# One ring of three PSUM slots, and one carry addition for two scans, in a selective-scan layer

## The chip, the core and the metric

The kernel runs on one core of one Trainium2 chip. A core has five engines with a queue of instructions each: PE (TensorE, matrix products, which writes to PSUM only), DVE (VectorE), ACT (ScalarE), POOL (GpSimd) and SP (SyncE, which here issues DMAs). Each engine works through its queue in order, and engines wait for each other by semaphores: an instruction may raise a count when it ends, and another may wait until the count has reached a value. The metric is the device time of one execution in microseconds (us).

The kernel is written in a language that records instructions and works out the semaphores itself, from which tiles an instruction reads and writes. Tiles come from pools: a pool with three buffers hands out three memory areas in turn, and a new tile waits until the last user of its area is done. Where the program asks for a manual schedule, the order on the engines named is the order of the code; elsewhere a scheduler orders them.

## What is computed

Four layers run one after the other on x (4 images of 64 x 64 pixels, 128 channels). The change is in layer 0, a state-space layer. Its heart is a scan over the 4096 pixels of an image, in four directions (rows, columns, and both backwards), for 256 inner channels with 16 states each:

```python
def step(h, inp):
    u_i, d_i, b_i, c_i = inp
    dA = jnp.exp(d_i[..., None] * A)
    h = h * dA + (d_i * u_i)[..., None] * b_i[:, None, :]
    y = jnp.einsum('gdn,gn->gd', h, c_i)
    return (h, y)
...
xs = jnp.stack([x_flat, x_t, jnp.flip(x_flat, 1), jnp.flip(x_t, 1)], axis=1)
...
ys = _selective_scan(xs, dts4, A, Bp4, Cp4, D_param, b_dt)
```

So h is multiplied by a decay dA and gets a product of the input (d times u) and b added; y sums h times c over the states. Ahead of it stand a group norm, a projection and a 3 x 3 convolution, behind it a layer norm, a gate and a projection.

## The kernel before

**Chunks and halves.** Layer 0 takes an image as 64 chunks of 64 steps, for two halves of the channels (128 each): 4 images x 2 halves x 64 chunks = 512 rounds of one loop (`for I in range(N)`). In a round c is the chunk's number, h the half. All four directions of a chunk are worked in the same round: j = 0, 1 (forwards, backwards) and kp = 0, 1 (rows, columns).

**One round** has two pairs, kp = 0 and kp = 1. For each:

- `products(q, kp)` (line 655) takes two PSUM tiles from the pool `db`, of 16 x 64 float32 a partition each (two PSUM banks), one for each j, and fills them with the products of `du` (d times u) and the diagonal tiles `dg` (b). These are 16 small matmuls on PE, which the trace shows as 32 records (two each): half 0 has four for j = 0 and then four for j = 1, then comes a drain of PE, then half 1 with four for j = 0 and four for j = 1. The tile of j = 0 is complete at the 12th matmul, that of j = 1 at the 16th.
- `scan(I, q, kp, bs, st, old, new)` (line 678), on DVE: for each j it adds the carry `old` (the last state of the chunk before, times the first decay) to the first of the 64 columns of the PSUM tile (line 684, 128 x 16 elements; not where c is 0), and runs the scan of 1024 elements (line 687) from the PSUM tile and the decays dA into `st` (tile `big` in SBUF). Then POOL makes the carry for the next round (line 694, `cy`) and multiplies both scans' states by c (line 702).

The pool `db` has three buffers (line 175), so the two tiles of the next pair get the third buffer and the one that the first scan of the present pair reads.

**Around it.** `inputs` (line 644) computes `du` on DVE for the next round. `total` (line 722) sums the states over n on PE, for the round two before; ACT copies the sums out (line 736). `diagonal` (line 636) and `decay` (line 591) make dg and dA on ACT. `beside` runs the other stages for the neighbouring images (`back`, `front`, `middle`, and `also` for layer 1's spectra), a step at a time, between the pairs; these use one PSUM tile of their own (`bg`).

**Order.** In the loop PE, ACT and DVE are under a manual schedule: PE has products (kp = 0), half of `total`, a step of `beside`, products (kp = 1), a step of `beside`, the other half of `total`; DVE has the scans (kp = 0), du, and what the step of `beside` has for it, the scans (kp = 1), and again a step. POOL and SP are ordered by the scheduler.

**Ahead of the loop** `front` and `middle` of image 0 run by themselves, ordered by the scheduler, and take their PSUM tiles one bank at a time from the same pool `db` (`turn_bank`, line 754).

Of the kernel before, what the change touches and what calls it, by code (L numbers as in the profile page):

```python
# [9 lines left out]
ALU = mybir.AluOpType  # L10
AX = mybir.AxisListType
PSUM = bass.MemoryType.PSUM
DRAM = bass.MemoryType.DRAM

P = 128
# [5 lines left out]
BLK = 512  # L21
# [6 lines left out]
TC = 64  # L28
NCHUNK = S // TC
NH0 = NST // 2  # L30
# [29 lines left out]
def tl(pool, shape, tag, dtype=F32, bufs=None):  # L60
    return pool.tile(shape, dtype, name=tag, tag=tag, bufs=bufs)
# [99 lines left out]
def layer0(cm, x, W, x1, also, kept):  # L161


    tc, nc = cm.tc, cm.nc
    wl = kept.enter_context(tc.tile_pool(name="l0k", bufs=1))
    dr = kept.enter_context(tc.tile_pool(name="l0dram", bufs=2, space=DRAM))
    with ExitStack() as ctx:
# [4 lines left out]
        t4 = ctx.enter_context(tc.tile_pool(name="l0t4", bufs=4))  # L172
        yb = ctx.enter_context(tc.tile_pool(name="l0y", bufs=2))
        p2 = ctx.enter_context(tc.tile_pool(name="l0p2", bufs=2))
        db = ctx.enter_context(tc.tile_pool(name="l0db", bufs=3, space=PSUM))
        pp = ctx.enter_context(tc.tile_pool(name="l0pp", bufs=1, space=PSUM))

        w_in = tl(wp, [P, 4 * P], "w_in")
# [58 lines left out]
        for i in range(2):  # L237
            t = tl(wp, [P, QC, 2, NH0, TC], f"dA{i}")
# [12 lines left out]
        for i in range(2):  # L251
            t = tl(wp, [P, 8, PADW], f"padded{i}")
            nc.vector.memset(t, 0.0)
            padded.append(t)
        for h in range(2):
            frame = xc_d[4 * h : 4 * h + 4].rearrange("g p s -> (g p) s")
            line = padded[h].rearrange("p r w -> p (r w)")
            nc.sync.dma_start(frame[:, 0:PADW], line[:, 0:PADW])
            nc.sync.dma_start(frame[:, (PADW - 1) * PADW :], line[:, 0 : PADW + 2])
        dg_d = tl(dr, [NCHUNK, P, NST * QR], "dg_d", bufs=1)  # L260

        img = {}
# [289 lines left out]
        def place(I):  # L552
            u, c = divmod(I, NCHUNK)
            return divmod(u, 2) + (c,)
# [100 lines left out]
            )  # L655

        def products(q, kp):
            bs = [tl(db, [P, 2 * NH0, TC], "db") for _ in range(2)]
            mm = None
            for half in range(2):  # L660
                if half:
                    nc.tensor.drain()
                for i in range(8):
                    j, r, p = i // 4, i // 2 % 2, i % 2
                    g = r ^ half
                    rows = slice((2 * j + r) * QR, (2 * j + r + 1) * QR)
                    t0 = (r ^ j) * QR
                    nc.tensor.matmul(  # L668
                        bs[j][
                            p * TC : (p + 1) * TC, g * NH0 : (g + 1) * NH0, t0 : t0 + QR  # L670
                        ],
                        lhsT=q["du"][rows, kp, g * TC : (g + 1) * TC],
                        rhs=q["dg"][rows, p * NH0 : (p + 1) * NH0, :],
                        start=True, stop=True,
                    )
            return bs

        def scan(I, q, kp, bs, st, old, new):
            c = q["c"]
            us = slice(2 * kp, 2 * kp + 2)  # L680
            for j in range(2):
                u = 2 * kp + j
                if c:
                    nc.vector.tensor_tensor(  # L684
                        bs[j][:, :, 0], bs[j][:, :, 0], old[:, u, :], ALU.add
                    )
                nc.vector.tensor_tensor_scan(  # L687
                    st[:, u].rearrange("p n t -> p (n t)"),
                    q["w"]["dA"][:, c % QC].rearrange("p g n t -> p (g n t)"),
                    bs[j].rearrange("p n t -> p (n t)"),  # L690
                    0.0, ALU.mult, ALU.add,
                )
            if c + 1 < NCHUNK:
                nc.gpsimd.tensor_tensor(  # L694
                    new[:, us, :], st[:, us, :, TC - 1],
                    quads[(I + 1) // QC]["a0"][:, (c + 1) % QC]
                    .rearrange("p g n -> p (g n)").unsqueeze(1)
                    .to_broadcast([P, 2, 2 * NH0]),
                    ALU.mult,
                )  # L700
            sv = st[:, us].rearrange("p j (g n) t -> p (j g) (n t)", g=2)
            nc.gpsimd.tensor_tensor(  # L702
                sv, sv,
                q["ct"].rearrange("p n t -> p (n t)").unsqueeze(1)
                .to_broadcast([P, 4, NH0 * TC]),
                ALU.mult,
            )

        def total(I, part):
# [36 lines left out]
            if c % (NCHUNK // 2) == NCHUNK // 2 - 1:  # L746
                for r in range(2):
# [3 lines left out]
                        ys[2].rearrange("p r w -> p (r w)")[:, rows], accum_op=ALU.add,  # L751
                    )

        def turn_bank():
            return tl(db, [P, BLK], "db")

        def own_bank():
            return tl(pp, [P, BLK], "bg")
# [5 lines left out]
        for _ in run(front(0, turn_bank), middle(0, turn_bank, t4, "t4k", 2)):  # L764
            pass
# [21 lines left out]
        with tc.manual_schedule(engines=engines):  # L787
            for I in range(N):
                b, h, c = place(I)
# [26 lines left out]
                if I + 1 < N:  # L816
                    nxt = start(I + 1)
                    diagonal(nxt)
                bs = products(now, 0)
                scan(I, now, 0, bs, st, carry, new)  # L820
                if nxt:
                    inputs(nxt)
# [5 lines left out]
                if w:  # L828
                    if c % QC == 1:
                        begun(w)  # L830
                    if c % QC == 2:
                        first(w)
                    decay(w, c % QC)
                bs = products(now, 1)
                scan(I, now, 1, bs, st, carry, new)
                if beside:
                    next(beside, None)
# [1432 lines left out]
def hybrid_kernel(tc, I, cst, out):  # L2270
    def part(prefix):
        return {k[len(prefix) :]: v for k, v in I.items() if k.startswith(prefix)}

    nc = tc.nc
    x = I["x"].rearrange("b r w c -> b (r w) c")
    out = out.rearrange("b r w c -> b (r w) c")
    with ExitStack() as ctx:
        cm = Common(ctx, tc, cst)
        dram = ctx.enter_context(tc.tile_pool(name="x1", bufs=1, space=DRAM))
        x1 = tl(dram, [B, S, D], "x1")  # L2280
        sp_d = tl(dram, [P, NT // UT, 5, UT, C], "sp_d")

        def also(*a):
            return spectra(cm, part("L1_conv_"), cst, sp_d, *a)

        xa = tl(dram, [B, S, D], "xa")
        xh_d = tl(dram, [B, S, D], "xh_d")
        lg_d = tl(dram, [P, 2, S], "lg_d")
        with ExitStack() as kept:
            last = layer0(cm, x, part("L0_conv_"), x1, also, kept)  # L2290
            recurrence_and_attention(
                cm, x1, part("L1_conv_"), part("L2_attn_"), part("L2_ffn_"), sp_d, xa, xh_d,
                lg_d, last,
            )
        x2 = tl(dram, [B, S, D], "x2")
        experts(cm, part("L2_ffn_"), xa, xh_d, lg_d, x2)
        layer3(cm, part("L3_attn_"), part("L3_ffn_"), cst, x2, out)
# [59 lines left out]
```

## Time and profile before

| What | us |
|---|---|
| Median of 3 runs | 10801.76 (10794.61 to 10804.73) |
| The profiled execution's own time | 10775.49 |
| Its span, first instruction to last | 10773.7 |
| DVE busy in the span | 7683.5 |
| PE busy in the span | 8887.1 |
| POOL busy in the span | 5462.3 |
| Scans (line 687), first to last start | 342.3 to about 6173 |

A trace's row names a line, an engine, an operation, the tile written and the tiles read, the shape and a count; behind it stand busy time and mean duration, or, in a timeline, start and duration in us. In square brackets, or behind the second bar, stands the idle time of the engine just before, with what ended it. Matmul records overlap in PE's pipeline, so their durations don't add up; what counts is when the first starts and when the engine behind it starts.

### The profile page before, as it was taken

To read this page: it belongs to the slowest core of one execution; us is meant where nothing else is said; L and a number is where in the kernel's file an instruction comes from. 1 tells how busy PE (TensorE), PEld (TensorE's weight loads), DVE (VectorE), ACT (ScalarE), POOL (GpSimd) and SP (SyncE) were. 2 spreads that over 40 slices of the span, in tenths; PEclk is the share of its full clock that TensorE was granted. 3 is DMA by queue.
4 is the path that set the end of the run, shared out by engine and by line. 5 is a ranking of instruction groups with operands and counts; after the bars stand their busy time and mean duration, and the time that the engine had idled before them with its cause. 6 is when DMAs were issued, how large, how long until landed. Compare 5 with 4: busy or idle time off the path is not lost. (4 is left out here: it accounts for less than half of the span.)

```text
span 10773.7 us, 190011 instructions
## 1 busy us (share of the span) xinstructions
PE 8887.1 (82%) x72040; PEld 4203.6 (39%) x72040; DVE 7683.5 (71%) x10667; ACT 5321.0 (49%) x13151; POOL 5462.3 (51%) x2661
## 2 busy tenths in 40 slices
PE   6678998779887788887788746999999956988886
PEld 2233443334333333333333323444444434544442
DVE  1699999999889999999999975636361132455546
ACT  5557554556444564445532124767676613433321
POOL 0579999889888888888999920000000000000000
PEclk7789998889888898888889868999999976687766
DMA  5434554335443344543333231111100083112101
GB/s 151 104 95 129 145 140 111 105 110 152 132 121 108 109 125 136 136 117 104 100 94 92 74 113 39 36 35 40 30 27 16 16 226 72 29 35 59 39 20 47
DMA packets 1155618, 960.91 MB, mean 89 GB/s; under 512 B 191940, under 2 KB 905384, under 8 KB 1148312
## 3 DMA queue, kind: packets, MB, share of 16 engines
q1 hardware_dynamic: 1140888, 898.41, 29.0%
q0 software_dynamic: 13824, 50.34, 2.6%
q8 instruction: 579, 9.49, 0.4%
q14 instruction: 327, 2.68, 0.1%
HBM read 616.68 MB, written 331.61 MB: 88 GB/s over the span
## 5 line engine op out<-in xcount | busy, mean ns | idle before, releaser
L687 DVE TENSOR_TENSOR_SCAN big<-dA,db 128x1024 f32<-128x1024 f32 x2048 | 4680.1, 2286 | 82.9 <-PE db L668 4.7
L702 POOL TENSOR_TENSOR big<-big,ct 128x2048 f32<-128x2048 f32 x1024 | 4653.7, 4545 | 78.8 <-POOL cy L694 0.4
L668 PE MATMUL db<-dg,du 32*64 32x256 f32 x32768 | 1914.5, 423 | 770.0 <-DVE db L684 625.4
L722 PE MATMUL yp<-big,both 128*64 128x256 f32 x16384 | 2368.4, 438 | 59.6 <-ACT yc L736 49.6
L722 PEld LDWEIGHTS yp<-big,both 128*64 128x64 f32 x16384 | 1250.5, 155 | 1158.8 <-issue 762.6
L668 PEld LDWEIGHTS db<-dg,du 32*64 32x64 f32 x32768 | 657.1, 136 | 2001.7 <-issue 1912.8
L736 ACT COPY yr<-yp 128x64 f32<-128x64 f32 x1024 | 224.6, 220 | 1538.0 <-PE yp L722 1537.6
L1480 PE MATMUL av<-e,x 128*128 128x512 f32 x2048 | 974.0, 592 | 4.6 <-ACT e L1475 4.6
L1431 PE MATMUL qk<-a,xT 128*128 128x512 f32 x2048 | 966.6, 594 | 8.7 <-ACT e L1435 7.9
L1435 ACT ACTIVATE e<-qk,nk 128x512 f32<-128x512 f32 x1024 | 694.0, 686 | 537.4 <-PE qk L1431 535.5
L591 ACT ACTIVATE dA<-dp,A 128x252 f32<-128x252 f32 x2048 | 869.6, 504 | 93.9 <-issue 48.7
L636 ACT ACTIVATE dg<-mask,BT 128x32 f32<-128x32 f32 x4096 | 902.2, 328 | 5.2 <-PE db L668 5.2
L1010 POOL TENSOR_TENSOR g_rs<-g_rs,qrow 128x4 f32<-128x4 f32 x32 | 41.2, 1286 | 1499.9 <-DVE g_rs L1009 1499.9
L694 POOL TENSOR_TENSOR cy<-big,a 128x32 f32<-128x32 f32 x1008 | 348.0, 345 | 467.3 <-DVE big L687 393.6
L1431 PEld LDWEIGHTS qk<-a,xT 128*128 128x128 f32 x2048 | 378.0, 190 | 462.4 <-issue 358.0
L1480 PEld LDWEIGHTS av<-e,x 128*128 128x128 f32 x2048 | 381.6, 190 | 434.8 <-issue 394.6
L1475 ACT ACTIVATE e<-e 128x1024 f32<-128x1024 f32 x510 | 539.4, 1058 | 15.4
L1956 ACT ACTIVATE e<-s 72x576 f32<-72x576 f32 x448 | 274.1, 643 | 494.2 <-PE s L1949 491.2
L684 DVE TENSOR_TENSOR db<-db,cy 128x16 f32<-128x16 f32 x2016 | 335.8, 167 | 209.7 <-PE db L668 174.5
L1967 POOL COPY vp<-vt 72x160 f32<-72x160 f32 x56 | 19.8, 354 | 889.0 <-PE po L1973 886.2
L2189 DVE SCALAR_TENSOR_TENSOR tex<-x,gw,tex 128x128 f32<-128x128 f32 x768 | 264.9, 345 | 259.5 <-PE x L2183 244.5
L1913 DVE TENSOR_REDUCE mx<-s 96x6 f32<-96x864 f32 x224 | 226.1, 1047 | 276.8 <-PE s L1905 276.6
(528 smaller groups left out, 9937.1 us busy)
## 6 DMA issues: line engine op xcount, KB each, us to landing
ct<-ct_d SPq DMA_DIRECT2D x1024, 128.0 KB
xo<-xT_d SPq DMA_DIRECT2D x2048, 32.0 KB
dg_d<-dg SPq DMA_DIRECT2D x256, 256.0 KB
dg<-dg_d SPq DMA_DIRECT2D x256, 256.0 KB
t4k<-xc_d SPq DMA_DIRECT2D x384, 132.0 KB
dT_d<-t2k SPq DMA_DIRECT2D x256, 128.0 KB
dp<-dl_d SPq DMA_DIRECT2D x256, 128.0 KB
dt<-dT_d SPq DMA_DIRECT2D x512, 64.0 KB
```

The source lines that it names most:

```text
L591: nc.scalar.activation(w["dA"][:, :, g, n, 1:], w["dp"][:, g, :, 1:], AF.Exp, scale=A[:, w["h"], g, n : n + 1],)
L636: nc.scalar.activation(q["dg"][:, n, :], mask, AF.Copy, scale=BT[:, q["c"], n : n + 1])
L668: nc.tensor.matmul(bs[j][p * TC : (p + 1) * TC, g * NH0 : (g + 1) * NH0, t0 : t0 + QR], lhsT=q["du"][rows, kp, g * TC : (g + 1) * TC], rhs ...
L684: nc.vector.tensor_tensor(bs[j][:, :, 0], bs[j][:, :, 0], old[:, u, :], ALU.add)
L687: nc.vector.tensor_tensor_scan(st[:, u].rearrange("p n t -> p (n t)"), q["w"]["dA"][:, c % QC].rearrange("p g n t -> p (g n t)"), bs[j].re ...
L694: nc.gpsimd.tensor_tensor(new[:, us, :], st[:, us, :, TC - 1], quads[(I + 1) // QC]["a0"][:, (c + 1) % QC] .rearrange("p g n -> p (g n)"). ...
L702: nc.gpsimd.tensor_tensor(sv, sv, q["ct"].rearrange("p n t -> p (n t)").unsqueeze(1) .to_broadcast([P, 4, NH0 * TC]), ALU.mult,)
L722: nc.tensor.matmul(yp[p * TC : (p + 1) * TC], lhsT=both, rhs=st[:, :, p * NH0 + n, :], start=(n == 0), stop=(n == NH0 - 1),)
L1431: nc.tensor.matmul(ps, lhsT=me["xT"][:, kt * P : (kt + 1) * P], rhs=me["a"][k], start=True, stop=True,)
L1435: nc.scalar.activation(e[:, j, :], ps, AF.Exp, bias=me["nk"][:, kt : kt + 1], scale=2.0)
L1475: nc.scalar.activation(es[g + 2], es[g + 2], AF.Exp)
L1480: nc.tensor.matmul(avs[b, k], lhsT=img[b]["x"][:, kt, :], rhs=e[:, j, :], start=(kt == 0), stop=(kt == NT - 1),)
```

## The change

The three buffers become one tile, `ring`, of three slots (six PSUM banks). The code works out itself which slots a pair uses: the k-th tile of a half image uses slot k mod 3, with k = 4 c + 2 kp + j, so pairs use slots (0, 1), (2, 0), (1, 2) and so on. The carry is added for both tiles of a pair in one instruction of 128 x 32 elements, ahead of both scans; where the pair lies in slots 2 and 0, its access pattern steps backwards. `turn_bank` hands out the ring's six banks in turn.

```diff
-        db = ctx.enter_context(tc.tile_pool(name="l0db", bufs=3, space=PSUM))
+        db = ctx.enter_context(tc.tile_pool(name="l0db", bufs=1, space=PSUM))
...
+        ring = tl(db, [P, 3, 2 * NH0, TC], "db")
...
         def products(q, kp):
-            bs = [tl(db, [P, 2 * NH0, TC], "db") for _ in range(2)]
+            k = 4 * q["c"] + 2 * kp
+            bs = [ring[:, (k + j) % 3] for j in range(2)]
...
         def scan(I, q, kp, bs, st, old, new):
             c = q["c"]
             us = slice(2 * kp, 2 * kp + 2)
+            if c:
+                k = (4 * c + 2 * kp) % 3
+                pair = ring[:, 2::-2, :, 0] if k == 2 else ring[:, k : k + 2, :, 0]
+                nc.vector.tensor_tensor(pair, pair, old[:, us, :], ALU.add)
             for j in range(2):
                 u = 2 * kp + j
-                if c:
-                    nc.vector.tensor_tensor(
-                        bs[j][:, :, 0], bs[j][:, :, 0], old[:, u, :], ALU.add
-                    )
                 nc.vector.tensor_tensor_scan(
...
+        banks = ring.rearrange("p s (g n) t -> p (s g) (n t)", g=2)
+        turn = [0]
+
         def turn_bank():
-            return tl(db, [P, BLK], "db")
+            turn[0] += 1
+            return banks[:, turn[0] % 6]
```

## The prediction

> **What bounds the kernel now.** I read the busy time by stretches first, then the costliest groups, then the timeline of one step, then the waits.
>
> ```profile
> core 0: us, PE busy (x) PEld busy (x) DVE busy (x) ACT busy (x) POOL busy (x), PEclk, DMA share, GB/s
> 342.00:6176.00 5834.00, 4837.30 (x52724) 2196.66 (x52712) 5529.98 (x4970) 2929.64 (x9426) 5206.50 (x2424) 0.89 0.41 115
> L687 DVE TENSOR_TENSOR_SCAN big<-dA,db 128x1024 f32<-128x1024 f32 x2048 | 4680.1, 2286 | 82.9 <-PE db L668 4.7
> L702 POOL TENSOR_TENSOR big<-big,ct 128x2048 f32<-128x2048 f32 x1024 | 4653.7, 4545 | 78.8 <-POOL cy L694 0.4
> L668 PE MATMUL db<-dg,du 32*64 32x256 f32 x32768 | 1914.5, 423 | 770.0 <-DVE db L684 625.4
> L684 DVE TENSOR_TENSOR db<-db,cy 128x16 f32<-128x16 f32 x2016 | 335.8, 167 | 209.7 <-PE db L668 174.5
> ```
>
> The first line names the columns of the second: the scan loop is the stretch from 342 to 6176 us. DVE is busy in 5530 of its 5834 us (95%), POOL in 5207, PE in 4837. The loop has 1024 pairs of scans (2048 scans), so a pair takes 5834/1024 = 5.70 us: DVE work, with hardly a wait for PE (175 us in all). DVE waits so little because PE runs ahead, as one step shows:
>
> ```profile
> 1511.15 2.29 DVE L687 TENSOR_TENSOR_SCAN big<-dA,db 128x1024 f32<-128x1024 f32 x1
> 1512.15 0.66 PE L668 MATMUL db<-dg,du 32*64 32x256 f32 x8
> 1513.35 0.16 DVE L684 TENSOR_TENSOR db<-db,cy 128x16 f32<-128x16 f32 x1
> 1513.55 2.29 DVE L687 TENSOR_TENSOR_SCAN big<-dA,db 128x1024 f32<-128x1024 f32 x1
> 1513.58 1.45 PE L668 MATMUL db<-dg,du 32*64 32x256 f32 x24 [0.77 <-DVE db L684]
> 1515.75 0.40 DVE L644 TENSOR_TENSOR du<-xo,dt 128x256 f32<-128x256 f32 x1
> ```
>
> While the first scan of a pair runs, PE writes a quarter of the next pair (8 of 32 records, 16 matmuls of two records each) into the third buffer. When that scan ends (1513.44), its buffer is free, PE goes on 0.14 us later, and the whole train is done under the second scan, at 1515.03, 0.7 us before DVE needs it.
>
> **The change part by part.** *The addition.* By the timeline, first scan to second scan is 2.40 us from start to start, and a scan to the following du 2.20: an addition between two scans costs 0.20 us. 1008 of 2016 go. The rest have 32 elements: from 167 ns at 16 elements to 696 ns at 512 (the addition in line 453) an element is 1.07 ns, so +17 ns each. Saved on DVE: 1008 x 0.18 = 182 us. The reversed step of one pair in three has no row; bounds 0 to +0.1 us on 336 pairs (the 0.12 by which an instruction that waits for the one before it starts later), 0 to 34 us; I take 0.
>
> *The waits.* The diff doesn't show them; the built program does. Before, the first matmul of a pair waits for the last scan of the pair before the previous one (or for du behind it), and the fifth matmul for the first scan of the previous pair, in 1018 of 1024 pairs. In the changed program the only DVE wait of a train is on its first matmul, and what it waits for is the *second* scan of the previous pair (again 1018 of 1024); the first scan of a pair no longer signals at all, the second signals for both. The pair's addition waits for the 16th matmul, where the first addition used to wait for the 12th. So all of a train now stands between the second scan of one pair and the addition of the next. Behind the waiting matmul, on PE, stand the train, the sums over states (line 722) and the interleaved work; behind the waiting addition, on DVE, two scans, then du. POOL and the ACT copies wait for these.
>
> *What the exposed train costs.* From scan end to first matmul: 0.14 us (above). From first matmul to the addition, these rows, in which DVE did wait for PE:
>
> ```profile
> 1102.68 0.69 PE L668 MATMUL db<-dg,du 32*64 32x256 f32 x16
> 1103.52 0.69 PE L668 MATMUL db<-dg,du 32*64 32x256 f32 x16 [0.15 <-issue]
> 1104.31 0.18 DVE L684 TENSOR_TENSOR db<-db,cy 128x16 f32<-128x16 f32 x1 [0.68 <-PE db L668]
> 428.29 1.16 PE L668 MATMUL db<-dg,du 32*64 32x256 f32 x16
> 429.60 1.16 PE L668 MATMUL db<-dg,du 32*64 32x256 f32 x16 [0.15 <-issue]
> 430.86 0.18 DVE L684 TENSOR_TENSOR db<-db,cy 128x16 f32<-128x16 f32 x1 [12.63 <-PE db L668]
> ```
>
> 1104.31 - 1102.68 = 1.63 us to the 12th matmul at full clock, 430.86 - 428.29 = 2.57 at the half clock that follows an idle PE. By the starts of the trace's records the 16th comes 0.27 (full) or 0.48 us (half) after the 12th: 1.90 and 3.05. A pair then takes 0.14 + train + addition 0.18 + 0.03 (gap to the scan) + 2.29 + 2.20 (the scans, the second overlapping by 0.08) = **6.74 us at full clock, 7.89 at half**. du (0.4) and most interleaved DVE work fall into DVE's wait of 2.0 to 3.2 us and cost nothing; without that cover, du would be 0.36 us a pair more. POOL's 5207/1024 = 5.08 a pair is covered by either period.
>
> *Which clock.*
>
> ```profile
> 342.00:366.00 24.00, 17.24 (x160) 5.81 (x156) 22.89 (x18) 5.25 (x21) 18.30 (x8) 0.50 0.37 120
> 800.00:960.00 160.00, 149.09 (x1584) 65.82 (x1582) 157.10 (x143) 138.96 (x433) 155.02 (x74) 0.98 0.47 144
> ```
>
> The last but two column is the granted clock: 0.50 at the loop's start, where PE runs short trains between pauses, 0.98 where it is 93% busy. In the trace the clock is full or half, and changes on a grid of 3.41 us: in the loop it fell after 95% of the full-clock stretches of that length in which PE was half busy, 73% of those 0.6 busy and 16% at 0.7, and it rose after 91% of the half-clock stretches that were fully busy and never at 0.7 or less. Of 25 trains that began after 2 to 3 us of idle PE, 22 ran at half clock. Now PE has, per pair at full clock, the train 1.53, the sums 1.95 and interleaved (4837 - 1914 - 2368)/1024 = 0.54 us: 4.0 of 6.74, its 2.7 us of idle in one piece ahead of the train. So it keeps falling. At half clock train 2.46 and sums 3.68 (the same groups where the clock was 0.5) with the rest doubled fill 7.2 of 7.89, so it soon rises. Half-clock pairs alternate with full-clock ones: I take one in three at half clock (bounds none and two in three): 6.74 + 1.15/3 = 7.12 us.
>
> The Trainium skill's page "TensorE: Matmul & The Clock Gate", section "Part 1: The HAM clock gate", says that the clock halves after a whole idle window of about 3.4 us. The grid agrees with the trace, the condition doesn't: here stretches half busy were enough. By the rule alone a pause of 2.7 us would leave the clock full and the loop at 6.74 us a pair.
>
> *What the cover can't hold.* 24 groups of the reciprocal in line 525 and its two products (3.34 + 2 x 0.68 = 4.7 us) exceed it by some 2.2 us, 53 us; eight like it in the spectra (lines 900, 901, 907), 20; 48 convolution steps on PE (line 376, 2.8 to 3.7 us) with the sums, about 1 us each, 50. Sum about 120 (bounds 40 and 250).
>
> *Ahead of the loop.* Lines 286 to 470 turn through six banks instead of three buffers, and the scheduler has moved SP's and ACT's order: loads of dp go up by seven blocks, xo ahead of the last dl and dT stores, the exponentials of dA among the second block's work with some more table loads. The first du waited 12.8 us for xo, and the products behind it could start where the last flip ends, at 330.5 instead of 339.7: at best -9 us. At worst ACT, which paces these blocks, takes 24 exponentials of 0.43 and four loads of 1.28: +15. I take 0.
>
> **Sum.** Loop 1024 x 7.12 = 7291, plus 120 = 7411, against 5834: +1577. On the profiled execution's own 10775.5 us (span 10773.7) that is 12352; the median of the runs, 10801.8, lies 26 above it: **12380 us**.
>
> **The rivals.** *A, the gain it reads like (faster):* DVE loses 182 us and PE's wait is met early, so that the train stays under the second scan: 10802 - 182 = 10620. For it: DVE is the busiest engine, and PE had 0.7 us to spare. It decides if a train's first matmul is seen starting before the previous pair's second scan ends. Against: that scan alone raises the count. The same skill's page "PSUM — Partial Sum Buffer", "Summary: rules for kernel authors", asks for guards by bank, and under such guards the slots would be as free as the three buffers were; the built program's waits say otherwise.
> *B, a cold loop:* more than two in three trains at half clock, 7.89 x 1024 + 250 = 8330, +2496: 13300. For it: the first 24 us. Against: a cold PE fills its stretches and warms.
> *C, a part hidden:* the wait is real, but a train costs about 1 us less than its rows (most pairs warm, and latencies overlapping): 5.8 to 6.6 us a pair, +100 to +960, so 10900 to 11760. Against: the rows have no such slack at full clock.
> *D, no change:* POOL, at 5.08 of 5.70 us, would have to set the period; its group waits for scans, not they for it (32 us in all): 10800.
>
> **How the numbers follow.** Forecast (mixed clock) 0.80, A 0.04, B 0.07, C 0.08, D 0.01. The low end is full clock throughout, 6.74 x 1024 + 40 - 5834 = +1108, 11900, lowered to 11800 for part of C; the high end two in three at half clock, (6.74 + 0.77) x 1024 + 250 - 5834 = +2106, 12900, raised to 12950 for part of B. Faster by over 0.2% (about what this measurement can tell from no change) is A, 0.04; within, 0.01; slower, the rest, 0.95.
>
> **What would show it.** Right: DVE's scans as long as before (2286 ns), 1008 additions of some 0.18 us, and behind most of them an idle time of 1.5 to 3 us with PE's train as releaser, some 2000 us in all; each train in one piece of 32 records, starting 0.14 us after a second scan; POOL's idle time before cy grown to 1.5 us and more a pair; a loop clock below 0.89. Wrong: trains that start under a second scan (A), idle of DVE that ends with POOL (D), a clock near 0.5 (B) or near 1 (low end).

## The result and the profile after

The changed kernel takes 12296.38 us (median; 12292.04 to 12318.25) against 10794.61 for the kernel before in the same comparison: a ratio of 1.1394 (95% interval 1.1379 to 1.141). It is slower, 84 us below the predicted time. The profiled execution has a span of 12291.4 us.

First the busy time by stretches, of the changed kernel (columns as in the prediction), cut where the first scan starts and the last one ends:

```profile
0.00:537.00 537.00, 290.65 (x1028) 101.93 (x1028) 47.09 (x100) 219.50 (x361) 1.59 (x10) 0.70 0.36 95
537.00:7697.00 7160.00, 5074.41 (x52706) 2215.71 (x52708) 5301.85 (x3962) 2930.91 (x9427) 5183.39 (x2424) 0.81 0.34 94
7697.00:12291.00 4594.00, 3834.47 (x18309) 1928.15 (x18304) 2106.29 (x5598) 2174.45 (x3367) 249.41 (x228) 0.84 0.20 52
```

and the stretch of the kernel before that the prediction did not show, ahead of its loop:

```profile
0.00:342.00 342.00, 206.55 (x1032) 82.91 (x1036) 46.85 (x99) 213.49 (x358) 1.60 (x10) 0.75 0.54 144
```

The loop has grown from 5834 to 7160 us (+1326) and the blocks ahead of it from 342 to 537 (+195). What follows the loop is unchanged (4597 before, 4594 now). In the loop DVE is busy for *less* time than before (5302 against 5530), and so is 74% busy instead of 95%: it waits. The costliest groups of the changed kernel name what for:

```profile
L689 DVE TENSOR_TENSOR_SCAN big<-dA,db 128x1024 f32<-128x1024 f32 x2048 | 4572.0, 2274 | 82.7 <-PE db L670 37.2
L670 PE MATMUL db<-dg,du 32*64 32x256 f32 x32768 | 1728.0, 482 | 2035.7 <-DVE big L689 1874.4
L686 DVE TENSOR_TENSOR db<-db,cy 128x32 f32<-128x32 f32 x1008 | 200.6, 199 | 1768.6 <-PE db L670 1695.3
L696 POOL TENSOR_TENSOR cy<-big,a 128x32 f32<-128x32 f32 x1008 | 315.0, 312 | 2092.9 <-DVE big L689 1716.9
```

The scans are about as long as they were (2274 ns against 2286). The additions are half as many, and ahead of them DVE now stands idle for 1769 us (210 before), released by the train of matmuls; the trains in turn stand idle for 2036 us (770 before), released by the scan. Two engines that release each other take turns. The timeline of three pairs of the changed kernel shows the turns (start, duration, engine; in brackets the idle time before and what ended it):

```profile
1809.50 1.53 PE L670 MATMUL db<-dg,du 32*64 32x256 f32 x32 [1.03 <-DVE big L689]
...
1811.19 0.20 DVE L686 TENSOR_TENSOR db<-db,cy 128x32 f32<-128x32 f32 x1 [1.42 <-PE db L670]
1811.42 4.47 DVE L689 TENSOR_TENSOR_SCAN big<-dA,db 128x1024 f32<-128x1024 f32 x2
...
1815.94 1.53 PE L670 MATMUL db<-dg,du 32*64 32x256 f32 x32 [1.98 <-DVE big L689]
...
1817.63 0.20 DVE L686 TENSOR_TENSOR db<-db,cy 128x32 f32<-128x32 f32 x1 [1.74 <-PE db L670]
1817.86 4.46 DVE L689 TENSOR_TENSOR_SCAN big<-dA,db 128x1024 f32<-128x1024 f32 x2
...
1822.38 2.47 PE L670 MATMUL db<-dg,du 32*64 32x256 f32 x32 [2.44 <-DVE big L689]
...
1825.00 0.20 DVE L686 TENSOR_TENSOR db<-db,cy 128x32 f32<-128x32 f32 x1 [2.36 <-PE db L670]
```

Two scans end at 1811.42 + 4.47 = 1815.89; 0.05 us later the whole train of 32 records runs; 1.69 us after its start comes the addition, and 0.23 us after that the next two scans. Nothing of a train lies under a scan any more. The third train took 2.47 us instead of 1.53: from 1822.38 to 1824.85 the granted clock was 0.50, under the first train it was 1.00.

Ahead of the loop, the waits (what waited for what: total us, times, longest us) of the changed kernel:

```profile
PE db L466 <- DVE t2k L455: 66.1, 8, 8.8
PE db L437 <- DVE t2k L455: 65.3, 8, 8.4
ACT t2k L387 <- PE db L377: 64.7, 16, 5.5
ACT t2k L444 <- PE db L437: 57.2, 14, 4.5
ACT padded L342 <- PE db L334: 34.6, 16, 2.2
ACT t2k L339 <- PE db L334: 33.3, 16, 2.2
```

and the same waits of the kernel before (its line numbers are lower by one):

```profile
PE db L465 <- DVE t2k L454: 45.5, 8, 6.5
ACT t2k L386 <- PE db L376: 41.1, 15, 8.1
ACT t2k L338 <- PE db L333: 12.3, 16, 1.2
ACT t2k L443 <- PE db L436: 8.1, 8, 1.3
ACT padded L341 <- PE db L333: 5.2, 16, 1.1
```

The second of the six has no counterpart before: TensorE's matmul of line 437 now waits for DVE's reading of another bank. It is the pattern of the loop again, with ACT and DVE as readers: a matmul into a bank waits until the reader of the bank *before* it has done, so nothing is prepared ahead. Longer matmuls come with it: for nearly the same number of records (1028 against 1032) TensorE is busy for 291 us instead of 207, at a granted clock of 0.70 instead of 0.75 in the mean. How much of the +195 is the clock, no run separates.

### The profile page after: what moved, and what is told of

The parts are those of the page before. It is cut to its first block, busy times and chain, and to the rows that moved or that the text cites. A ratio compares the mean times of both kernels' runs of the same rounds, so it can differ in the third digit from the quotient of the medians.

```text
span 12291.4 us, 187636 instructions
## 1 busy us (share of the span) xinstructions
PE 9199.5 (75%) x72040; PEld 4245.8 (35%) x72040; DVE 7455.2 (61%) x9659; ACT 5324.9 (43%) x13155; POOL 5434.4 (44%) x2661
## 5 line engine op out<-in xcount | busy, mean ns | idle before, releaser
L689 DVE TENSOR_TENSOR_SCAN big<-dA,db 128x1024 f32<-128x1024 f32 x2048 | 4572.0, 2274 | 82.7 <-PE db L670 37.2
L670 PE MATMUL db<-dg,du 32*64 32x256 f32 x32768 | 1728.0, 482 | 2035.7 <-DVE big L689 1874.4
L724 PE MATMUL yp<-big,both 128*64 128x256 f32 x16384 | 2610.3, 473 | 25.1 <-ACT yc L738 22.0
L724 PEld LDWEIGHTS yp<-big,both 128*64 128x64 f32 x16384 | 1335.9, 168 | 1327.6 <-issue 1028.3
L670 PEld LDWEIGHTS db<-dg,du 32*64 32x64 f32 x32768 | 556.7, 151 | 3185.2 <-DVE big L689 1865.2
L686 DVE TENSOR_TENSOR db<-db,cy 128x32 f32<-128x32 f32 x1008 | 200.6, 199 | 1768.6 <-PE db L670 1695.3
L696 POOL TENSOR_TENSOR cy<-big,a 128x32 f32<-128x32 f32 x1008 | 315.0, 312 | 2092.9 <-DVE big L689 1716.9
```

The source lines that it names most:

```text
L670: nc.tensor.matmul(bs[j][p * TC : (p + 1) * TC, g * NH0 : (g + 1) * NH0, t0 : t0 + QR], lhsT=q["du"][rows, kp, g * TC : (g + 1) * TC], rhs ...
L689: nc.vector.tensor_tensor_scan(st[:, u].rearrange("p n t -> p (n t)"), q["w"]["dA"][:, c % QC].rearrange("p g n t -> p (g n t)"), bs[j].re ...
L724: nc.tensor.matmul(yp[p * TC : (p + 1) * TC], lhsT=both, rhs=st[:, :, p * NH0 + n, :], start=(n == 0), stop=(n == NH0 - 1),)
```

## The experiments

Theory T, from the two traces: whatever fills any slot or bank of the one tile is made to wait for the last reader of the whole tile, in the loop (+1326) and ahead of it (+195) alike. Rivals: R1, it is the pair's addition, which needs the last matmul of both slots, that takes TensorE and DVE apart; R2, it is the rotation by hand with the order of loads and exponentials that came with it; R3, about the size only: much of the loss is the clock, which falls because TensorE pauses. Ratios are to the kernel before, with 95% intervals.

**Rotation by hand, but three tiles.**

```diff
-        ring = tl(db, [P, 3, 2 * NH0, TC], "db")
+        ring = [tl(db, [P, 2 * NH0, TC], f"db{i}") for i in range(3)]
...
-            bs = [ring[:, (k + j) % 3] for j in range(2)]
+            bs = [ring[(k + j) % 3] for j in range(2)]
```

(and an addition ahead of each scan again, and `turn_bank` over the six halves of the three tiles; "..." stands for code left out)

> The rotation by hand stays as in the changed kernel (slot by pair number, six banks in turn ahead of the loop), but the three slots are three tiles, and each scan has its own addition again. Theory T (one tile is guarded as one piece, so that everything that fills any slot waits for the last reader of the whole tile): the loop is back at about 5833 us and the part ahead of the first scan at about 342, in all 10795, give or take 30; the loop's idle of DVE ahead of the additions is some 200 us instead of 1769. Rival R2 (the rotation by hand, and the order of loads and exponentials that comes with it, is what costs): time stays near 12290, at least ahead of the loop (+194, so 10990).

Measured: 10796.27 us, 1.0006 (0.9995 to 1.0016); loop 5852 us, first scan at 337. Its groups:

```profile
L670 PE MATMUL db<-dg,du 32*64 32x256 f32 x32768 | 1911.3, 427 | 781.2 <-DVE big L689 592.2
...
L686 DVE TENSOR_TENSOR db<-db,cy 128x16 f32<-128x16 f32 x2016 | 335.6, 166 | 202.3 <-PE db L670 166.8
```

The idle times are close to those of the kernel before (770 and 210 us). Turning slots and banks by hand costs nothing that can be told from noise: R2 falls.

**One tile, single additions.**

```diff
-            if c:
-                k = (4 * c + 2 * kp) % 3
-                pair = ring[:, 2::-2, :, 0] if k == 2 else ring[:, k : k + 2, :, 0]
-                nc.vector.tensor_tensor(pair, pair, old[:, us, :], ALU.add)
             for j in range(2):
                 u = 2 * kp + j
+                if c:
+                    nc.vector.tensor_tensor(
+                        bs[j][:, :, 0], bs[j][:, :, 0], old[:, u, :], ALU.add
+                    )
```

> The changed kernel with only the pair's addition undone: one tile as ring, one addition ahead of each scan. T: the wait is that of the tile, so the train stays behind the second scan; an addition of 0.17 us more and the gap between the scans come back, 0.20 us a pair, against which the first addition of the pair has to wait for 12 of 16 matmuls only (0 to 0.3 us less): 12200 to 12500, with the part ahead of the first scan at 537 us. Rival R1 (the pair's addition, which waits for the last matmul of both slots, is what takes PE and DVE apart): near 10800 to 11000, with trains under the second scan again.

Measured: 12542.13 us, 1.163 (1.1604 to 1.1657), first scan at 533. Without the pair's addition the kernel is even slower than the changed one, so that instruction is not what costs; in itself it earns 246 us inside the ring. R1's condition is not taken away by this run, though: the first addition starts 1.69 us after the start of its train (median), as the pair's addition does, so it too waits for the last matmul, and not for the 12th only, as I had expected. R1 is decided by two runs further down. The time lies 42 us above T's range: from first to second scan it is 2.54 us, 0.14 more than in the kernel before, which I hadn't counted. The second addition now waits for the scan just ahead of it (the same tile) and starts 0.035 us after its end, where before it started 0.083 us ahead of that end.

**Half of the change each: ring in the loop only, ring ahead of it only.**

```diff
+        with tc.tile_pool(name="l0fr", bufs=3, space=PSUM) as fr:
+            def turn_bank():
+                return tl(fr, [P, 2 * NH0, TC], "fr").rearrange("p n t -> p (n t)")[:, 0:BLK]
+            for _ in run(front(0, turn_bank), middle(0, turn_bank, t4, "t4k", 2)):
+                pass
+        db = ctx.enter_context(tc.tile_pool(name="l0db", bufs=1, space=PSUM))
+        ring = tl(db, [P, 3, 2 * NH0, TC], "db")
```

> Ring and pair addition in the scan loop only; the blocks ahead of it use a pool of three buffers of their own, closed before the loop. T: first scan near 342 us instead of 537, the loop as slow as in the changed kernel (7160 us): 12100, give or take 40. Rival R2 (the 194 us ahead of the loop come from the changed order of loads and exponentials, or from the carry's addition): stays near 12290. A third outcome, the loop's period changing by more than 2% from 6.99 us, would say that what runs ahead reaches into the loop.

The second kernel is the one before, with `turn_bank` of the change over a ring in a pool of its own:

```diff
+        with tc.tile_pool(name="l0fr", bufs=1, space=PSUM) as fr:
+            ring = tl(fr, [P, 3, 2 * NH0, TC], "fr")
+            banks = ring.rearrange("p s (g n) t -> p (s g) (n t)", g=2)
...
+        db = ctx.enter_context(tc.tile_pool(name="l0db", bufs=3, space=PSUM))
```

> The other half: the loop as before the change (three buffers, an addition for each scan), and only the blocks ahead of it turn through the six banks of one tile. T: first scan near 537 us, loop 5833 us, in all 10990, give or take 20, so that this run and the one with the ring in the loop only add up to the whole change (194 + 1327 of 1518 us). Rival R2 (the order of SP and ACT, moved by the scan's new form, is what costs ahead of the loop): near 10800.

Measured: 12122.4 us, 1.1232 (1.1192 to 1.1271), and 10995.78 us, 1.0185 (1.0161 to 1.0209). Stretches ahead of the loop and of the loop, of the kernel with the ring in the loop only:

```profile
0.00:343.00 343.00, 207.66 (x1028) 83.24 (x1028) 46.87 (x99) 213.42 (x358) 1.60 (x10) 0.75 0.54 143
343.00:7509.00 7166.00, 5076.22 (x52714) 2217.07 (x52710) 5296.44 (x3962) 2931.95 (x9427) 5187.44 (x2424) 0.81 0.34 94
```

and of the kernel with the ring ahead of it only:

```profile
0.00:534.00 534.00, 287.72 (x1036) 100.69 (x1036) 47.09 (x100) 219.41 (x361) 1.59 (x10) 0.72 0.36 96
534.00:6385.00 5851.00, 4846.95 (x52710) 2204.55 (x52704) 5536.36 (x4970) 2923.58 (x9427) 5200.87 (x2423) 0.88 0.41 115
```

The second run's ratio is clear of noise, if small. Each half carries its own loss, 1332 and 206 us over the kernel before in the same comparison; their sum, 1538, is within 40 us of the whole, 1502. What happens ahead of the loop does not reach into it.

**Both additions first, in three tiles.** From the first experiment's kernel:

```diff
             for j in range(2):
-                u = 2 * kp + j
                 if c:
                     nc.vector.tensor_tensor(
-                        bs[j][:, :, 0], bs[j][:, :, 0], old[:, u, :], ALU.add
+                        bs[j][:, :, 0], bs[j][:, :, 0], old[:, 2 * kp + j, :], ALU.add
                     )
+            for j in range(2):
+                u = 2 * kp + j
                 nc.vector.tensor_tensor_scan(
```

> Three tiles turned by hand, and both additions of a pair put ahead of both scans, so that DVE waits for the last matmul of both slots as the pair addition does, but no tile holds two slots. T: no wait for the whole tile, so the train stays under the scans: between 10740 and 10830 (DVE's work is the same; the second addition moves). R1 (it is the waiting for the last matmul of both slots that takes PE and DVE apart): some part of the 1327 us of the loop comes back, 11200 or more.

Measured: 10666.55 us, 0.9876 (0.9857 to 0.9896): faster than the kernel before, by more than T's range said. R1 falls, since here too DVE waits for the last matmul of both slots before it scans, and 959 of 1023 trains start before the previous pair's second scan ends (972 before the change, none after it). Why it is faster is taken up below.

**The ring by slot.** The kernel with the ring in the loop only, in which the waits of each matmul are those of its own slot:

```diff
+                    slot = (k + j) % 3
+                    for slots, user in users:
+                        if slot not in slots:
+                            tc.declare_no_dep(mm.ins, user.ins, reason="other slots")
+                    own = [user for slots, user in users if slot in slots]
+                    if own:
+                        after(mm, own[-1])
```

(`users` holds the latest scans and additions with the slots that they touch; each of them is made to wait for the last matmul of its pair)

> Ring tile and pair addition in the loop as in the changed kernel, the blocks ahead of it on a pool of their own as before the change; and the waits of each train are written by slot: the waits that the tile's guard gives for scans and additions of other slots are taken off, and each matmul waits for the last scan or addition that reads its own slot (the reversed pair addition counts as one of all three slots). T: the pair addition itself is cheap and does what the diff reads like: trains run under the second scan again, DVE is spared some 0.18 us a pair, 10570 to 10700 (the price given to rival A was 10620). R1 (one addition that needs the last matmul of both slots costs the loop its overlap whatever the guards): above 11000. In between, 10750 to 10850: the spared 182 us go to another engine, POOL first (5.08 us of work a pair against 5.52).

Measured: 10714.45 us, 0.992 (0.9906 to 0.9935). The tile, the rotation and the pair's addition are all there, and only the false waits of the trains are gone: 1408 us less than with the ring in the loop. This is T shown at its cause, and R1 falls again. The trains lie under scans again:

```profile
1514.48 0.20 DVE L696 TENSOR_TENSOR db<-db,cy 128x32 f32<-128x32 f32 x1
...
1514.71 4.47 DVE L700 TENSOR_TENSOR_SCAN big<-dA,db 128x1024 f32<-128x1024 f32 x2
...
1516.13 0.66 PE L670 MATMUL db<-dg,du 32*64 32x256 f32 x8
...
1517.05 1.46 PE L670 MATMUL db<-dg,du 32*64 32x256 f32 x24 [0.26 <-DVE big L700]
```

8 records of the train run under the first scan and 24 under the second, as before the change; 941 of 1023 trains start before the previous pair's second scan ends. But the gain is some 80 us, just short of what I expected, and not the 182 that the prediction gave to rival A.

**The same with six one-bank tiles ahead of the loop.**

```diff
-        with tc.tile_pool(name="l0fr", bufs=3, space=PSUM) as fr:
+        with tc.tile_pool(name="l0fr", bufs=6, space=PSUM) as fr:
-                return tl(fr, [P, 2 * NH0, TC], "fr").rearrange("p n t -> p (n t)")[:, 0:BLK]
+                return tl(fr, [P, BLK], "fr")
```

> The same loop, and the blocks ahead of it turn through six tiles of one bank each instead of three of two banks (what the ring's six banks read like). T: as the run with waits by slot, less what more buffers bring ahead of the loop: 0 to 30 us (ACT is busy for 137 us of the first 342 and TensorE for some 185, so buffers are hardly what those blocks wait for). Rival: the six banks do cost something by the changed order of loads, 10 to 40 us more.

Measured: 10707.04 us, 0.9918 (0.9903 to 0.9932), first scan at 344 instead of 348. Not to be told from three buffers. (The expectation's 137 us of ACT and 185 of TensorE are those of the changed kernel's first 334 us; before the change they are 213 and 207 of 342.)

**Keeping TensorE busy.** The changed kernel, with work added:

```diff
+            for n in range(4 * part, 4 * part + 4):
+                for p in range(2):
+                    nc.tensor.matmul(
+                        yp[p * TC : (p + 1) * TC], lhsT=none,
+                        rhs=st[:, :, p * NH0 + n, :], start=False, stop=(n == NH0 - 1),
+                    )
```

> The changed kernel with extra work for TensorE: each matmul of the sums over states is issued a second time with zero weights, which adds nothing to the sums and keeps TensorE busy under the scans. Theory on the size (R3: of the 6.99 us of a pair, the trains at half clock, 35% of them at some 0.93 us more, are 0.33 us): the clock stays above 0.95 in the loop, hardly a train runs at half clock, a pair takes 6.44 to 6.7 us and the whole some 300 us less than the changed kernel, 11900 to 12100. If instead the clock is no cause of it (the slow pairs are late for another reason, such as the work interleaved on DVE), or TensorE's work itself becomes too long for the two scans, the time stays or grows: 12290 or more.

Measured: 12218.29 us, 1.1315 (1.1296 to 1.1335). Its loop:

```profile
533.00:7584.00 7051.00, 5929.12 (x69012) 3116.18 (x69014) 5298.33 (x3962) 2930.74 (x9427) 5200.51 (x2424) 0.96 0.34 96
```

The clock did what was asked (0.96; 3% of the trains at half clock instead of 35%), but the loop gained only 109 us of the 300 expected. The two traces together say why. In the changed kernel 363 pairs with a half-clock train take 7.43 us in the mean, the other 660 take 6.76: 363 x 0.67 = 243 us is an estimate of what the clock costs. In this run trains that start over 0.3 us after the second scan's end, since TensorE is still at earlier work, are 224 instead of 113, and their lateness sums to 268 us instead of 136. Taken pair by pair, the 345 pairs whose train went from half to full clock became 212 us shorter, although their trains start 32 us later in all; the 649 at full clock in both became 101 longer, 91 of it trains that start later. The few others hardly change. So R3 holds in kind, with some 240 us, of which the added work gives back more than half; the expectation was wrong to price that work at nothing. 41 us more behind the loop (4635 against 4594) are left unexplained.

**Where the spared DVE time goes.** To see why additions first gain 1.2% and the ring by slot only 0.8%, I sorted the pairs by what stands on DVE between one pair's scans and the next pair's: nothing ("direct", 425 pairs), or du alone (403). Medians of the time from pair to pair in us, worked out from the scans' starts in each trace:

| | direct | with du | whole loop |
|---|---|---|---|
| before | 4.80 | 5.25 | 5833 |
| ring by slot | 4.83 | 5.04 | 5769 |
| additions first | 4.64 | 5.28 | 5727 |

In direct pairs the ring by slot saves nothing at all. Its addition waits for the scan just ahead of it (false too: another slot of the same tile): where it follows a scan directly it starts 0.134 us after the scan's end (median), where before it started 0.083 ahead of that end. Its first scan starts 0.034 after the addition, as it did before. With the additions first, the first one overlaps the scan ahead of it, the second one the first and the scan the second, and both additions together take 0.20 us from the first one's start to the scan's. So I added only the addition's wait for the scan (`last[0]` is the scan issued last):

```diff
+                    if j == 0:
+                        after(add, last[0])
```

> The kernel with three tiles and both additions first (0.9876 of before), in which the first addition of each pair is also made to wait for the scan that stands just before it on DVE, though that scan reads another tile; the ring by slot has this wait left in it by the tile's guard. Theory S (the ring by slot stayed at 0.992 instead of going below 0.983, because what DVE saves by one addition less is given back where an instruction waits for the one just ahead of it: it starts 0.035 us after the end instead of 0.083 before it): half of the additions follow a scan directly (du or interleaved work stands ahead of the others), 504 x 0.12 = 60 us at most, less where POOL holds the pair: 10690 to 10730, near the ring by slot. Rival (the 32-element addition, or TensorE's later start in the ring by slot, makes the difference): no change, 0.9876, about 10666.

Measured: 10683.32 us, 0.9887 (0.987 to 0.9903). The mark is in the trace (direct pairs: median 4.82, fastest tenth 4.816 instead of 4.578), but the loop is as long as without (5727 us both times): theory S fails on the time. Summed up, the 425 direct pairs became 71 us longer, and the pairs with du (403 with du alone, 108 with du and other work) 74 us shorter. Something else takes up what DVE is spared. The timeline of the additions-first kernel shows POOL without a pause:

```profile
1515.34 0.27 POOL L697 TENSOR_TENSOR cy<-big,a 128x32 f32<-128x32 f32 x1
1515.69 4.55 POOL L705 TENSOR_TENSOR big<-big,ct 128x2048 f32<-128x2048 f32 x1
1520.19 0.45 POOL L697 TENSOR_TENSOR cy<-big,a 128x32 f32<-128x32 f32 x1
1520.72 4.54 POOL L705 TENSOR_TENSOR big<-big,ct 128x2048 f32<-128x2048 f32 x1
```

and in the same stretch, on DVE:

```profile
1519.73 0.79 DVE L645 TENSOR_TENSOR du<-xo,dt 128x256 f32<-128x256 f32 x1
```

That du ends at 1520.52, 0.28 us after POOL's large multiplication (1520.24). It is no single case: of the 317 du in this trace that started at least 0.13 us before the end of such a multiplication, 316 ended 0.26 to 0.30 us after its end, and the 149 that started with POOL idle all took 0.40 us. So du waits until POOL's multiplication is done, and DVE, whose next scans stand behind du, can't run ahead of POOL.

A pair needs 4.85 us or more of POOL (1515.34 to 1520.19), more than DVE's 4.58. POOL begins a pair with less than 0.1 us of idle time in 75% of the pairs (50% in the kernel before). So two more kernels cut POOL's large multiplication to three of the four parts of a pair (the product of the fourth is left out; the broadcast of c is cut to fit), without and with the extra wait:

```diff
-            sv = st[:, us].rearrange("p j (g n) t -> p (j g) (n t)", g=2)
+            sv = st[:, us].rearrange("p j (g n) t -> p (j g) (n t)", g=2)[:, 0:3]
```

> The kernel with three tiles and both additions first, and POOL's large multiplication (states times C, 4.55 us a pair) is done for three of the four parts of a pair only; the product of the fourth part is left out, to take POOL off the bound. Theory P (with the additions first, POOL, which starts its next pair without idle time in 75% of the pairs, takes up the rest of what DVE is spared: 0.22 us a pair by DVE's own steps, 222 us, of which 106 came out in the loop): with POOL's pair cut from 4.85 to some 3.7 us, the loop falls by 100 us or more below 5727, and du's mean from 877 ns to below 550: in all 10350 to 10560. Rival (PE or DVE holds the loop): 10600 to 10670.

> The same cut of POOL's multiplication (the product of the fourth part is left out), in the kernel whose first addition also waits for the scan just before it. With POOL holding the pairs, that wait cost nothing in the loop (5727 us with and without). Theory P: without POOL's hold its 0.24 us in the pairs whose addition follows a scan directly (425 of 1023; 4.816 against 4.578 us) come out: 60 to 110 us slower than the other kernel of this pair. Rival (the wait is hidden behind TensorE's trains in any case): less than 30 us apart.

Measured: 10480.08 us, 0.971 (0.9693 to 0.9726), loop 5534; and 10528.75 us, 0.9763 (0.9741 to 0.9784), loop 5576. Without the wait, the two groups to look at are:

```profile
L705 POOL TENSOR_TENSOR big<-big,ct 128x1536 f32<-128x1536 f32 x1024 | 3537.1, 3454 | 92.2 <-DVE big L690 10.7
...
L697 POOL TENSOR_TENSOR cy<-big,a 128x32 f32<-128x32 f32 x1008 | 325.9, 323 | 1240.0 <-DVE big L690 891.6
```

POOL now idles 1240 us ahead of cy (374 with its full work), the loop loses 193 us, and du's mean falls from 877 to 503 ns. Theory P holds: POOL held the loop, and it did so through du. The pairs with du became 207 us shorter, of which du's own time is 192; the direct pairs did not become shorter (2129 and 2142 us in all). The wait now costs 42 us in the loop and 49 in the time, more than the 30 of its rival and less than the 60 that P said at least: the direct pairs became 56 us longer, and the pairs with du give back 12 instead of 74. Why the direct pairs lose 56 and not the 100 that 425 x 0.24 would be, I did not trace.

**Additions first, with the pool's own buffers.** The kernel before, with the additions moved ahead as above and six one-bank tiles ahead of the loop:

```diff
+            for j in range(2):
+                if c:
+                    nc.vector.tensor_tensor(
+                        bs[j][:, :, 0], bs[j][:, :, 0], old[:, 2 * kp + j, :], ALU.add
+                    )
```

> The kernel before, with three buffers from its pool in the loop, both additions of a pair ahead of both scans, and six buffers of one bank ahead of the loop. If the rotation by hand has no part in the gain (theory T, with S for where it comes from): 0.9876 of before, less 0 to 10 us ahead of the loop: 10650 to 10680. If rotation by hand brings some of it: above 10700.

Measured: 10676.42 us, 0.988 (0.9863 to 0.9898), as with three tiles turned by hand. The gain is the order of the additions; no ring is needed. These two kernels beat both the kernel before and the changed one.

## Why the prediction was right, and where not

*The mechanism* was right, and the run with the waits written by slot shows it: the tile's guard, not the addition, is what exposes the train. Rival A's condition, a train that starts under the previous pair's second scan, occurs with the ring only where the waits are by slot (941 of 1023 trains; none in the changed kernel). The Trainium skill's page "PSUM — Partial Sum Buffer", section "Summary: rules for kernel authors", asks for guards by bank; the runs agree that such guards (here by slot, of two banks) are enough and that a guard of the whole tile is 1408 us dearer.

*"Ahead of the loop ... I take 0"* is the step that failed: it measured +195 us, far outside its bounds of -9 and +15. I had read the built program's waits for the loop's trains only, and looked ahead of the loop at the queues' order alone. The same guard holds there, bank after bank; the timeline of the changed kernel shows TensorE (L471, L466) and ACT (the copies of L476) taking turns:

```profile
179.05 2.08 PE L471 MATMUL db<-t2k,flip 128*128 128x512 f32 x2 [0.67 <-ACT t2k L476]
...
181.16 0.59 ACT L476 COPY t2k<-db 128x512 f32<-128x512 f32 x1 [2.17 <-PE db L471]
...
181.80 1.11 PE L466 MATMUL db<-ident,t2k 128*128 128x128 f32 x4 [0.68 <-ACT t2k L476]
182.95 0.59 ACT L476 COPY t2k<-db 128x512 f32<-128x512 f32 x1 [1.20 <-PE db L466]
...
183.59 2.08 PE L471 MATMUL db<-t2k,flip 128*128 128x512 f32 x2 [0.67 <-ACT t2k L476]
```

*The loop's terms* were mis-sized by 251 us the other way (+1577 against +1326), so that the two errors nearly cancel in the total: that it is only 84 us off is luck in good part. (The other 25 us: the median of the runs lies 3 us above the profiled execution, where I added 26.) The pair at full clock: 6.74 predicted, 6.44 measured. The wait from scan to train is 0.055 us instead of 0.14, and the train up to the addition 1.69 instead of 1.90 (2.62 instead of 3.05 at half clock). The 0.14 was a misreading: the row names the second scan's addition as what released the train, and that ended at 1513.51, 0.07 us before; in the run with three tiles, where the scan releases it, the wait is 0.055. I had added the spacing of the record starts, 0.27 us, for the 16th matmul after the 12th; the addition came just 0.06 later than the rows for the 12th give. Over 1024 pairs that is some -310 us. One train in three at half clock, a choice between wide bounds, was 35.5%, at 0.94 us each by the medians instead of 1.15: some 340 us for 393. And what the cover can't hold, 120 us with bounds 40 and 250, is 7160 - 1024 x 6.437 - 340 = 229: 136 us of it trains that TensorE's other work made late, which I had as 50, the rest by subtraction the groups that I listed, which I did not trace one by one. Only the sum of these last two terms, 569 us, is firm: with the clock at the 243 us that the means of the pairs give, the cover's share would be 326, above its bound.

*The saving on DVE* was 0.18 us a pair. Within the ring, where a single addition also waits for the scan ahead of it, it is more (246 us between single and pair additions, 0.24 a pair). As the price of rival A, 10620, it was wrong: with slots free for TensorE (the addition's own false wait for the scan stays) the pair addition gives 10714. The price left out that an instruction which waits for its predecessor starts later, although the prediction has such a figure (0.12 us; here it is 0.134 + 0.083 = 0.22) for the reversed step alone. It also left out that POOL, at 5.08 of 5.70 us in the mean, already starts half of its pairs without a pause, and that du waits for POOL's multiplication. I dismissed POOL in rival D by its mean and by its idle time's releasers; this wait shows as a longer du and not as idle time. (Rival C's upper end is a slip of arithmetic: 6.6 x 1024 - 5834 is +924 and not +960.)

*What would show it:* 1008 additions (199 ns), trains in one piece of 32 records, 1769 us of idle DVE ahead of the additions (some 2000 expected), POOL's idle time before cy at 1717 us for scans (1.70 a pair), a loop clock of 0.81. All as listed but the 0.14; 58% of the additions have an idle time of 1.5 to 3 us ahead of them, most of the others less.

## What to carry to other kernels

Merging the buffers of a rotation into one tile merges their guards: read the built program's waits of *every* stage that uses the tile, not only the one that the change is about, or write the waits by slot. If an addition or other small step stands between two long instructions that depend on it, put two independent small steps side by side ahead of both, which costs hardly more than one and spares the waits for the predecessor; but price what DVE is spared only as far as the next engine (here POOL, which du waits for) has a pause in the same pairs, not in the mean.

## What the runs showed of the hardware beyond this

DVE's instructions overlap: one that needs nothing of its predecessor starts 0.083 us before that one's end, one that waits for it 0.035 after, on 167 ns additions as on 2.27 us scans; the first additions that wait for the scan ahead of them in the ring by slot start 0.134 after. du, 0.40 us beside an idle POOL, ends 0.28 us after the POOL multiplication beside which it starts: 0.88 in the mean where POOL ran almost without a pause, 0.72 in the kernel before and 0.47 in the changed kernel, where POOL idles. And the clock fell for 35% of the trains though TensorE's pauses in the pairs shown were 1.0 to 2.4 us long; keeping it busy with work of no use lifted the clock to 0.96 and gave back more than half of the some 240 us that this brought.
